# Fourier mixing with three real products for four: a spectral layer's weight stage rewritten

## The chip, the cores and the metric

One core of a Trainium2 chip runs the whole program. Its engines work side by side and meet through semaphores: TensorE (PE, matmul, with its weight loads listed apart as PEld), VectorE (DVE), ScalarE (ACT), GpSimd (POOL) and SyncE (SP, which here only issues transfers). The metric is the device time of one execution in microseconds (us); lower is better.

## What is computed

The input is x, 4 batches of 512 times, 128 positions (n) and 64 channels (c), all in float32. Two layers follow each other. Layer 0 (normalisations, a scan, convolutions, a feed-forward block) is not touched. Layer 1, cut to what matters:

```
trend = _moving_average(x, 25)
seasonal = x - trend
xf = rfft(seasonal, axis=time)
xs = xf[:, :128]
W = w_real + 1j * w_imag
ys = einsum('bmnc,cmk->bknc', xs, W)
filt = irfft(ys padded with zeros, n=512)
return trend + filt
```

The `einsum` is the mixing. For each of the 64 channels a complex 128 x 128 matrix W[c] takes the 128 spectral modes m to 128 modes k, for every batch and position. With X = Xr + iXi and W = A + iB the plain form needs four real products: Yr = A.Xr - B.Xi and Yi = B.Xr + A.Xi.

## The kernel before

Layer 1 takes the batches in two pairs (G = 2). For each pair it runs three stages, one after the other: `transform` of both batches (moving average and forward Fourier transform as matmuls), `mix`, and `invert` of both (inverse transform, with the trend added and the result stored). Between the stages lies one large tile, `xf`, with 128 partitions of spectrum; per batch it has two planes r = 0, 1 of 64 x 128 columns. It is permuted so that a fixed channel's columns can be read as matmul input: for one channel, 2 batches x 64 x 2 = 256 columns, in runs of two neighbouring elements.

The spectrum is packed by symmetry classes of the modes. `MODES` lists modes 0, 4, 8, ... (32 of them), then 2, 6, 10, ... (32), then the odd ones (64). After `transform`, plane 0 holds the real parts in this order; plane 1 holds the imaginary parts with its halves turned, the odd modes first (`IMAG` is `MODES` rolled by half). After `mix`, plane 0 holds the even modes in four blocks of 32 (real, imaginary, real, imaginary) and plane 1 the odd ones in two blocks of 64; this packed order is what `invert` multiplies.

`transform` (L987) goes through 16 slabs of 512 columns in 8 groups of two. Per group: loads on SP, sums and differences on VectorE (L1006 to L1010), three small copies to `edge` on ScalarE (L1002), then matmuls L1018 (128 x 64 weights), L1026 (128 x 32 weights, four of them side by side in the array's columns) and L1035, then four ScalarE copies of PSUM to `xf` (L1042).

`mix` (L1044) goes through 16 groups of four channels (CG = 4). Per group it loads 1 MB of weights: for each channel two 128 x 128 matrices for each of two output planes, already arranged on the host so that plane 0 and plane 1 of `xf` are each multiplied once into each output plane. GpSimd flips the signs of a part of them (L1053, two instructions of 128 x 256). Then TensorE runs 16 matmuls of 128 x 128 weights and 256 columns (L1060 and L1064, four per channel), two at a time summed in PSUM, and VectorE and ScalarE copy the sums back over the spectrum in `xf` (`evacuate`, L962 to L966), two instructions of 128 x 256 each per two channels.

`invert` (L1076) goes through 16 slabs per batch, `waves(s)` ahead of `trends(s - 1)`: matmuls L1086 and L1088 into four PSUM banks, VectorE sums L1094 and L1098, then matmuls L1114 and L1117 and four VectorE sums L1120, and a store from GpSimd's queue (L1121).

TensorE's order is the program's order (`manual_schedule`); the order on the other engines is made by a planner when the program is built. Every float32 matmul stands in the profile as two instructions, so 512 matmuls of the two `mix` stages are 1024 rows. Buffers bind the stages: the `big` pool has five slots of 8 KB per partition, used in turn by input slabs (`xin`) and by weights (`w`); PSUM has eight banks of 512 columns, tag "a" with four and tag "b" with four.

The lines that bind most:

```
1044  def mix(xf):
1049      w = slabs.tile([P, CG, 2, 2, M], F32, tag="big", name="w", bufs=5)
1050      nc.sync.dma_start(w, wri[:, g * CG : (g + 1) * CG, :, :, :])
1056      py = [bank("b"), bank("b")]
1129  with tc.manual_schedule(engines={nc.tensor.engine}):
1134      mix(xf)
```

Of the kernel before, what the change touches and what calls it, by code (L numbers as in the profile page):

```python
# [31 lines left out]
TURN = 16  # L32

MODES = np.concatenate([np.arange(0, M, 4), np.arange(2, M, 4), np.arange(1, M, 2)])
IMAG = np.roll(MODES, H)

HALVES = np.arange(D).reshape(-1, 2, 2, 2, H)
HALVES[:, 1] = HALVES[:, 1, :, ::-1].copy()
# [880 lines left out]
def layer1(ctx, tc, x4, wri, dftv, dftd, dfte, idfte, idfto, avg, avgh, out, after):  # L919
# [41 lines left out]

    def evacuate(i, dst, src):  # L962
        if i % 2:
            nc.scalar.copy(dst, src)
        else:
            nc.vector.tensor_copy(dst, src)  # L966

    def slab(b, s):
        xin = slabs.tile([P, NT, SL], F32, tag="big", name="xin", bufs=5)
# [17 lines left out]
    def transform(b, xf):  # L987

        for g in range(NS // 2):
            edge = io.tile([P, SL], F32, tag="edge", name="edge")  # L990
            uv, ev, pf = [], [], []
            for k in range(2):
                s = 2 * g + k
                c = slice(s * SL, (s + 1) * SL)
                with behind(b, s, after["sync"][min(s, 4) + 2]):
                    xin = shifted_slab(b, s)
                ends = xin[0 : 2 * TURN, 0, :]
                if k == 0:
# [8 lines left out]
                nc.vector.tensor_tensor(u, xin[:, 0:2, :], xin[:, 2:4, :], ALU.add)  # L1007
                t = io.tile([P, 2, SL], F32, tag="ev", name="ev")
                for i, op in enumerate((ALU.add, ALU.subtract)):
                    nc.vector.tensor_tensor(t[:, i, :], u[:, 0, :], u[:, 1, :], op)  # L1010
                uv.append(v)
                ev.append(t)
                pf.append([bank("ab"[g % 2]), bank("ab"[g % 2])])
            for k in range(2):
                for i in range(2):
                    for r in range(2):
                        h = 1 - r
                        nc.tensor.matmul(  # L1018
                            pf[k][r][h * H : (h + 1) * H, :], lhsT=dftd_sb[:, i, r, :], rhs=uv[k][:, i, :],
                            start=(i == 0), stop=False,  # L1020
                        )
            for k in range(2):
                for i in range(2):
                    for r in range(2):
                        q = r * H + i * H // 2
                        nc.tensor.matmul(  # L1026
                            pf[k][r][q : q + H // 2, :], lhsT=dftv_sb[:, i, r, :], rhs=ev[k][:, i, :],
                            start=True, stop=False,
                        )
            for k in range(2):  # L1030
                for r in range(2):
                    at = slice(k * H + 32 * r, k * H + 32 * r + 2 * TURN)
                    for h in range(2):
                        hs = slice(h * H, (h + 1) * H)
                        nc.tensor.matmul(  # L1035
                            pf[k][r][hs, :], lhsT=dfte_sb[at, hs], rhs=edge[at, :] if k + r else first,
                            start=False, stop=True,
                        )
            for k in range(2):
                s = 2 * g + k  # L1040
                for r in range(2):
                    nc.scalar.copy(by_c(xf[:, r, s * SL : (s + 1) * SL]), by_n(pf[k][r]))  # L1042

    def mix(xf):  # L1044

        xc = xf.rearrange("p b r (a c l) -> p b r a c l", c=H, l=2)
        for g in range(H // CG):

            w = slabs.tile([P, CG, 2, 2, M], F32, tag="big", name="w", bufs=5)
            nc.sync.dma_start(w, wri[:, g * CG : (g + 1) * CG, :, :, :])  # L1050
            w4 = w[:, :, 1, 0, :].rearrange("p c (n i m) -> p c n i m", n=2, i=2)[:, :, :, 0, :]
            for t in (w4, w[:, :, 1, 1, 0:H]):
                nc.gpsimd.tensor_scalar(t, t, -1.0, 0.0, ALU.mult, ALU.add)  # L1053
            for q in range(CG // 2):
                c0 = g * CG + 2 * q
                py = [bank("b"), bank("b")]
                for r in range(2):
                    for j in range(2):
                        o = py[r][:, j * G * NF : (j + 1) * G * NF]
                        nc.tensor.matmul(  # L1060
                            o, lhsT=w[:, 2 * q + j, 0, r, :], rhs=xc[:, :, 0, :, c0 + j, :], start=True,
                            stop=False,
                        )
                        nc.tensor.matmul(  # L1064
                            o, lhsT=w[:, 2 * q + j, 1, r, :], rhs=xc[:, :, 1, :, c0 + j, :],
                            start=False, stop=True,
                        )
                for r in range(2):
                    for b in range(G):
                        evacuate(  # L1070
                            b,
                            xc[:, b, r, :, c0 : c0 + 2, :],
                            py[r].rearrange("p (c b a l) -> p b a c l", c=2, b=G, l=2)[:, b],
                        )

    def invert(b, xf):  # L1076

# [2 lines left out]
        def waves(s):  # L1080

            c = slice(s * SL, (s + 1) * SL)
            ev, od = [bank("a"), bank("a")], [bank("a"), bank("a")]
            for h in range(2):
                hs = slice(h * H, (h + 1) * H)
                nc.tensor.matmul(ev[h], lhsT=idfte_sb[hs, :], rhs=xf[hs, 0, c], start=True, stop=True)  # L1086
            for i in range(2):
                nc.tensor.matmul(od[i], lhsT=idfto_sb[:, i, :], rhs=xf[:, 1, c], start=True, stop=True)  # L1088
            even = io.tile([P, 2, SL], F32, tag="ev", name="even")
            two = io.tile([P, SL], F32, tag="even", name="two")  # L1090
            nc.scalar.copy(two, ev[1])  # L1091
            halves[s] = []
            for i, op in enumerate((ALU.add, ALU.subtract)):
                nc.vector.tensor_tensor(even[:, i, :], ev[0], two, op)  # L1094
            for i in range(2):
                pm = (slabs if i else io).tile([P, 2, SL], F32, tag=f"uv{i}", name="pm")
                for k, op in enumerate((ALU.add, ALU.subtract)):
                    nc.vector.tensor_tensor(pm[:, k, :], even[:, i, :], od[i], op)  # L1098
                halves[s].append(pm)

        def trends(s):
# [3 lines left out]
            for j in range(NT):  # L1105
# [22 lines left out]

    with tc.manual_schedule(engines={nc.tensor.engine}):
        for b0 in range(0, B, G):  # L1130
            xf = spec.tile([P, G, 2, D], F32, tag="xf", name="xf")
            for b in range(G):
                transform(b0 + b, xf[:, b, :, :])
            mix(xf)
            for b in range(G):
                invert(b0 + b, xf[:, b, :, :])


def _constants():
# [43 lines left out]
def _inputs(x, i):  # L1183
# [18 lines left out]
            wconv[sa, q, 2 * H :] = taps[2 - 2 * a]  # L1202


    planes = []
    for rows, parts in ((MODES, ("w_real", "w_imag")), (IMAG, ("w_imag", "w_real"))):
        w = [i[n][:, rows][..., MODES] for n in parts]
        planes += [[v[..., q : q + H // 2] for q in (0, H // 2) for v in w], [v[..., H:] for v in w]]
    wri = np.stack([np.concatenate(p, axis=2) for p in planes], axis=2)
    b = x.shape[0]  # L1210
    a = {
        "x": x.reshape(b, T, D),
# [11 lines left out]
        "wri": wri.reshape(H, M, 2, 2, M).transpose(1, 0, 2, 3, 4),  # L1224
        **_constants(),
    }
    return {n: np.ascontiguousarray(v) for n, v in a.items()}
# [17 lines left out]
```

## Time and profile before

| | us |
|---|---|
| median of 3 runs | 3674.95 (3670.21 to 3675.77) |
| the profiled execution | 3668.25 |
| its span (first to last instruction) | 3666.5 |
| first `mix`: first matmul to the first matmul of `invert` | 2816.30 to 2927.74 |
| second `mix`: the same | 3298.44 to 3409.9 |
| first `transform` stage, its matmuls | 2699.4 to 2814.0 |
| first `invert` stage, its matmuls | 2927.7 to 3172.9 |

Over the whole span TensorE is busy for 94%, VectorE 74%, ScalarE 49% and GpSimd 12%. These shares are averages over stages with different limits, so the stages are looked at one by one. In the tables of groups, a row gives line, engine, operation, output and inputs, shapes, count, then busy time in us and the mean duration of one in ns, then the idle time before them and what ended it. In the timeline a row gives the start, the duration of the whole run of equal instructions, and the count after "x". A matmul's duration is longer than the distance to the next one, because matmuls are pipelined: for what a stage costs, the distance between starts counts.

### The profile page before, as it was taken

The numbers are of one execution on the slowest core, as the hardware profiler recorded it, in microseconds if no ns is written. First come the engines' busy times: TensorE is split into PE (matmuls) and PEld (weight loads), VectorE is DVE, ScalarE is ACT, GpSimd is POOL, SyncE is SP. The second block draws the span as 40 slices with busy tenths as digits, with TensorE's granted clock in tenths as the row PEclk, the third lists the DMA queues.
The fourth block names the chain that finished last, engine by engine and source line by source line (L and its number), as shares of the span: only waits on it lengthen the run. The fifth ranks groups of instructions, "written<-read, shape, count | busy, mean of one in ns | idle before, by whom it ended". The sixth has DMA issues, their size and how long they took to land. (4 is left out here: it accounts for less than half of the span.)

```text
span 3666.5 us, 53980 instructions
## 1 busy us (share of the span) xinstructions
PE 3458.3 (94%) x20297; PEld 1363.8 (37%) x20297; DVE 2707.6 (74%) x3530; ACT 1787.3 (49%) x2363; POOL 448.6 (12%) x657
## 2 busy tenths in 40 slices
PE   8989998889998899999899989999999999999998
PEld 3433332234333223433322333343334833328433
DVE  4476779976776996677699799956677277892677
ACT  0013445655666565666656688878864200252100
POOL 0000012210111211010122121100001000001000
PEclk9999999999999999999999999999999999999999
DMA  9876657787885788788478678646668478994688
GB/s 314 288 260 232 225 187 257 257 280 269 288 275 174 265 275 289 271 282 282 164 264 284 214 255 266 227 169 213 233 197 266 149 254 289 300 302 148 224 281 263
DMA packets 427732, 910.48 MB, mean 248 GB/s; under 512 B 32848, under 2 KB 83664, under 8 KB 423376
## 3 DMA queue, kind: packets, MB, share of 16 engines
q1 hardware_dynamic: 353904, 637.11, 53.3%
q0 software_dynamic: 71680, 268.46, 20.3%
q8 instruction: 162, 2.65, 0.3%
q10 hardware_dynamic: 1888, 1.45, 0.1%
q14 instruction: 98, 0.80, 0.1%
HBM read 638.39 MB, written 268.50 MB: 247 GB/s over the span
## 5 line engine op out<-in xcount | busy, mean ns | idle before, releaser
L780 PE MATMUL p<-mid,w_sb 64*64 64x512 f32 x2048 | 551.5, 596 | 17.6 <-DVE wx L793 17.6
L780 PE MATMUL pb<-mid,w_sb 64*64 64x512 f32 x2048 | 534.0, 596 | 0.0
L770 ACT ACTIVATE mid<-c,fb_sb 128x1024 f32<-128x1024 f32 x256 | 284.3, 1111 | 93.0 <-PE c L765 90.8
L770 ACT ACTIVATE mid<-m,fb_sb 128x1024 f32<-128x1024 f32 x256 | 284.6, 1112 | 92.0 <-PE m L765 90.8
L765 PE MATMUL c<-x,w_sb 64*64 64x512 f32 x2016 | 279.0, 606 | 12.8 <-ACT mid L770 6.5
L765 PE MATMUL m<-x,w_sb 64*64 64x512 f32 x2016 | 283.0, 613 | 7.4 <-ACT ob L814 5.0
L780 PEld LDWEIGHTS p<-mid,w_sb 64*64 64x64 f32 x2048 | 154.1, 134 | 291.9 <-issue 262.1
L1091 ACT COPY two<-a 128x512 f32<-128x512 f32 x64 | 37.5, 585 | 432.0 <-PE a L1086 432.0
L414 PE MATMUL a<-xp,wx 128*128 128x512 f32 x512 | 235.2, 603 | 0.5 <-DVE me L269 0.5
L1114 PE MATMUL b<-xin,avg_sb 128*128 128x512 f32 x512 | 230.8, 593 | 3.3 <-DVE xin L1120 3.3
L1120 DVE TENSOR_TENSOR xin<-b,pm 128x512 f32<-128x512 f32 x256 | 159.1, 683 | 101.3 <-PE b L1117 86.3
L601 ACT ACTIVATE sq<-x 128x1024 f32<-128x1024 f32 x128 | 135.0, 1055 | 156.9 <-DVE x L596 156.8
L252 PE MATMUL st<-x,ones 128*32 128x512 f32 x512 | 185.2, 611 | 24.5 <-DVE x L596 24.5
L656 DVE SCALAR_TENSOR_TENSOR to<-kd,vec,to 128x511 f32<-128x511 f32 (+1 forms) x272 | 196.9, 742 | 10.4 <-ACT to L652 8.1
L733 ACT ACTIVATE kd<-kd,vec 128x512 f32<-128x512 f32 x256 | 192.7, 803 | 3.1 <-DVE kd L725 3.1
L966 DVE COPY xf<-b 128x256 f32<-128x256 f32 x128 | 54.3, 424 | 179.0 <-PE b L1060 170.0
L542 DVE TENSOR_TENSOR x<-a,xp 128x1024 f32<-128x1024 f32 x128 | 156.0, 1219 | 38.2 <-PE a L538 35.6
L656 DVE SCALAR_TENSOR_TENSOR z<-x,vec,z 128x511 f32<-128x511 f32 x240 | 175.6, 744 | 5.0 <-ACT z L652 3.6
L736 DVE TENSOR_TENSOR x<-kd,kx 128x1024 f32<-128x1024 f32 x126 | 154.0, 1222 | 33.4 <-ACT kd L733 33.4
L538 PE MATMUL a<-rst,wo_sb 64*64 64x512 f32 x1024 | 143.3, 627 | 27.5 <-DVE x L542 25.2
L793 DVE SCALAR_TENSOR_TENSOR x4t<-p,fb_sb,x 128x512 f32<-128x512 f32 x64 | 47.7, 746 | 160.0 <-PE pb L780 157.6
L724 DVE TENSOR_TENSOR kd<-kh,rm 128x1024 f32<-128x1024 f32 x128 | 155.6, 1219 | 7.1 <-ACT rm L286 4.6
(275 smaller groups left out, 6773.5 us busy)
## 6 DMA issues: line engine op xcount, KB each, us to landing
xp<-in_xt SPq DMA_DIRECT2D x256, 512.0 KB
kh<-to SPq DMA_DIRECT2D x156, 512.0 KB
x<-x POOLq DMA_DIRECT2D x128, 512.0 KB, 4.4
kx<-x SPq DMA_DIRECT2D x128, 512.0 KB
x<-ob POOLq DMA_DIRECT2D x64, 1024.0 KB, 8.1
xin<-x SPq DMA_DIRECT2D x64, 1024.0 KB
out<-xin POOLq DMA_DIRECT2D x64, 1024.0 KB, 6.3
x<-x SPq DMA_DIRECT2D x96, 512.0 KB
```

The lines of the kernel that those rows point to most:

```text
L252: nc.tensor.matmul(st[32 * q : 32 * q + 32, :], lhsT=ones, rhs=src[:, j, :], start=first, stop=last,)
L414: nc.tensor.matmul(pa[:, k, :], lhsT=wq[:, j, k * P : (k + 1) * P], rhs=xp[:, j, :], start=first and j == 0, stop=last and j == 1,)
L542: nc.vector.tensor_tensor(x1, at, xp, ALU.add)
L656: tap = nc.vector.scalar_tensor_tensor(to[:, j, k:], xr[:, j, : SL - k], vec[:, w, c], to[:, j, k:], ALU.mult, ALU.add)
L724: nc.vector.tensor_tensor(d, to, pair_of(rb), ALU.mult)
L733: tc.keep_in_program_order(nc.scalar.activation(d[:, j, :], d[:, j, :], AF.Identity, bias=vec[:, B4, c], scale=vec[:, G4, c]))
L736: nc.vector.tensor_tensor(x3, d, x2, ALU.add)
L765: nc.tensor.matmul(pm[halves[j], h, :], lhsT=w1_sb[halves[h], q * H : (q + 1) * H], rhs=x3[halves[h], j, :], start=True, stop=True,)
L770: gelu = nc.scalar.activation(mid, pm, AF.Gelu_apprx_tanh, bias=fb1_sb[:, q : q + 1])
L780: nc.tensor.matmul(sums2[i][j][halves[h], :], lhsT=w2_sb[halves[j], q, :], rhs=mid[halves[j], h, :], start=q == 0, stop=q == 3,)
L1114: nc.tensor.matmul(po[j], lhsT=avg_sb[:, j, :], rhs=xin[:, j, :], start=True, stop=False)
L1120: nc.vector.tensor_tensor(by_n(xin[:, j, :]), by_n(po[j]), by_c(pm[j % 2][:, j // 2, :]), ALU.add)
```

## The change

The complex product is written with three real products per channel: with d = Xr - Xi (formed by VectorE), B.d is common to both results, and (A - B).Xr + B.d = Yr and (A + B).Xi + B.d = Yi. The parts, in words:

- The host gives the two real planes of W only, 512 KB per group of four channels. GpSimd forms A - B and A + B into two further planes of the same tile (two instructions of 128 x 512 per group), in place of the sign flips.
- `xf` holds the real part in plane 0 and the imaginary part in plane 1, with modes in the same order in both; the order of its dimensions becomes plane, batch, column. `transform`'s last copies turn the halves of plane 1: one ScalarE copy of 128 partitions and two of 64 per slab, for two of 128.
- `mix` has four steps per group: `load_weights`, `differ` (d, one VectorE instruction of 128 x 1024 elements), `common` (four matmuls with 128 x 128 weights, then five ScalarE copies and one VectorE copy that lay the result out in the packed order, as `first` and `other`) and `own` (32 matmuls with 128 x 32 weights, each to 32 partitions of PSUM, in sets of four that differ in these partitions, then two VectorE sums of 128 x 1024 which write `xf` in the packed order that `invert` reads). They are issued so that `common` of the next group stands ahead of `own` of this one.
- PSUM is taken in pairs of banks everywhere in layer 1 (`banks`, two per tag, for `bank`, four per tag), so two neighbouring banks are taken and given back together.

```diff
-    ps = ctx.enter_context(tc.tile_pool(name="ps", bufs=4, space=PSUM))
+    ps = ctx.enter_context(tc.tile_pool(name="ps", bufs=2, space=PSUM))
...
-    def bank(tag):
-        return ps.tile([P, SL], F32, tag=tag, name=tag)
+    def banks(tag):
+        return ps.tile([P, 2, SL], F32, tag=tag, name=tag)
...
                 s = 2 * g + k
-                for r in range(2):
-                    nc.scalar.copy(by_c(xf[:, r, s * SL : (s + 1) * SL]), by_n(pf[k][r]))
+                c = slice(s * SL, (s + 1) * SL)
+                nc.scalar.copy(by_c(xf[:, 0, c]), by_n(pf[k][:, 0, :]))
+                for h in range(2):
+                    rows, turned = slice(h * H, (h + 1) * H), slice((1 - h) * H, (2 - h) * H)
+                    nc.scalar.copy(by_c(xf[rows, 1, c]), by_n(pf[k][turned, 1, :]))
...
+        def by_a(block):
+            return block.rearrange("p k (c a l) -> p a (k c) l", c=2, l=2)
+
+        def load_weights(g):
+            w = ws[g] = slabs.tile([P, 4, CG, M], F32, tag="big", name="w", bufs=5)
+            nc.sync.dma_start(w[:, 0:2], wri[:, g])
+            nc.gpsimd.tensor_tensor(w[:, 2], w[:, 0], w[:, 1], ALU.subtract)
+            nc.gpsimd.tensor_tensor(w[:, 3], w[:, 0], w[:, 1], ALU.add)
+
+        def differ(g):
+            d = ds[g] = slabs.tile([P, CG, G * NF // 2, 2], F32, tag="uv1", name="d")
+            c = channels(g)
+            nc.vector.tensor_tensor(d.rearrange("p c a l -> p a c l"), xc[:, 0, :, c, :], xc[:, 1, :, c, :], ALU.subtract)
+
+        def common(g):
+            w, d = ws[g], ds.pop(g)
+            pk = banks("a")
+            for c in range(CG):
+                nc.tensor.matmul(
+                    pk[:, c // 2, c % 2 * G * NF : (c % 2 + 1) * G * NF], lhsT=w[:, 1, c, :], rhs=d[:, c], start=True, stop=True
+                )
+            first = io.tile([P, 2, SL], F32, tag="uv0", name="first")
+            other = io.tile([P, 2, SL], F32, tag="ev", name="other")
+            q = H // 2
+            for at in range(4):
+                nc.scalar.copy(first[at * q : (at + 1) * q], pk[at // 2 * q : (at // 2 + 1) * q])
+            nc.scalar.copy(other[0:H], pk[H:P])
+            nc.vector.tensor_copy(other[H:P], pk[H:P])
+            turns[g] = first, other
+
+        def own(g):
+            w = ws.pop(g)
+            q = H // 2
+            parts = (((0, 0), (1, 0), (0, 1), (1, 1)), ((0, 2), (0, 3), (1, 2), (1, 3)))
+            py = [banks("b"), banks("b")]
+            for k in range(2):
+                for c in range(CG):
+                    for at, (r, m) in enumerate(parts[k]):
                         nc.tensor.matmul(
+                            py[k][at * q : (at + 1) * q, c // 2, c % 2 * G * NF : (c % 2 + 1) * G * NF],
+                            lhsT=w[:, 2 + r, c, m * q : (m + 1) * q], rhs=xc[:, r, :, g * CG + c, :],
+                            start=True, stop=True,
                         )
+            for k, turn in enumerate(turns.pop(g)):
+                nc.vector.tensor_tensor(xc[:, k, :, channels(g), :], by_a(py[k]), by_a(turn), ALU.add)
+
+        for g in range(3):
+            load_weights(g)
+        differ(0)
+        common(0)
+        differ(1)
+        for g in range(NG):
+            if g + 3 < NG:
+                load_weights(g + 3)
+            if g + 1 < NG:
+                common(g + 1)
+            if g + 2 < NG:
+                differ(g + 2)
+            own(g)
...
-            ev, od = [bank("a"), bank("a")], [bank("a"), bank("a")]
+            ev, od = banks("a"), banks("a")
...
-            po = [bank("b") for _ in range(NT)]
+            pairs = [banks("b"), banks("b")]
+            po = [pairs[j // 2][:, j % 2, :] for j in range(NT)]
```

More of the change, by code (lines that the diff above doesn't have):

```diff
@@ L960, in by_n @@
         return row.rearrange("p (a l c) -> p a l c", c=H, l=2)
[L962 to L966, printed above, removed]
     def slab(b, s):
@@ L1012, in transform @@
                 ev.append(t)
-                pf.append([bank("ab"[g % 2]), bank("ab"[g % 2])])
+                pf.append(banks("ab"[g % 2]))
             for k in range(2):
@@ L1035, in transform @@
                         nc.tensor.matmul(
-                            pf[k][r][hs, :], lhsT=dfte_sb[at, hs], rhs=edge[at, :] if k + r else first,
+                            pf[k][hs, r, :], lhsT=dfte_sb[at, hs], rhs=edge[at, :] if k + r else first,
                             start=False, stop=True,
@@ L1040, in transform @@
                 s = 2 * g + k
-                for r in range(2):
-                    nc.scalar.copy(by_c(xf[:, r, s * SL : (s + 1) * SL]), by_n(pf[k][r]))
-    def mix(xf):
[L1046 to L1059, printed above, removed]
+                c = slice(s * SL, (s + 1) * SL)
@@ L1082, in waves @@
             c = slice(s * SL, (s + 1) * SL)
-            ev, od = [bank("a"), bank("a")], [bank("a"), bank("a")]
+            ev, od = banks("a"), banks("a")
             for h in range(2):
                 hs = slice(h * H, (h + 1) * H)
-                nc.tensor.matmul(ev[h], lhsT=idfte_sb[hs, :], rhs=xf[hs, 0, c], start=True, stop=True)
+                nc.tensor.matmul(ev[:, h, :], lhsT=idfte_sb[hs, :], rhs=xf[hs, 0, c], start=True, stop=True)
             for i in range(2):
-                nc.tensor.matmul(od[i], lhsT=idfto_sb[:, i, :], rhs=xf[:, 1, c], start=True, stop=True)
+                nc.tensor.matmul(od[:, i, :], lhsT=idfto_sb[:, i, :], rhs=xf[:, 1, c], start=True, stop=True)
             even = io.tile([P, 2, SL], F32, tag="ev", name="even")
             two = io.tile([P, SL], F32, tag="even", name="two")
-            nc.scalar.copy(two, ev[1])
+            nc.scalar.copy(two, ev[:, 1, :])
             halves[s] = []
             for i, op in enumerate((ALU.add, ALU.subtract)):
-                nc.vector.tensor_tensor(even[:, i, :], ev[0], two, op)
+                nc.vector.tensor_tensor(even[:, i, :], ev[:, 0, :], two, op)
             for i in range(2):
@@ L1130, in layer1 @@
         for b0 in range(0, B, G):
-            xf = spec.tile([P, G, 2, D], F32, tag="xf", name="xf")
+            xf = spec.tile([P, 2, G, D], F32, tag="xf", name="xf")
             for b in range(G):
-                transform(b0 + b, xf[:, b, :, :])
+                transform(b0 + b, xf[:, :, b, :])
             mix(xf)
             for b in range(G):
-                invert(b0 + b, xf[:, b, :, :])
+                invert(b0 + b, xf[:, :, b, :])
 def _constants():
@@ L1202, in _inputs @@
             wconv[sa, q, 2 * H :] = taps[2 - 2 * a]
[L1205 to L1209, printed above, removed]
+    wri = np.stack([i[n][:, MODES][..., MODES] for n in ("w_real", "w_imag")], axis=1)
     b = x.shape[0]
```

27 lines of the change are left out of this document (9 added, 18 removed).

## The prediction

> **What bounds the kernel now.** I read the busy shares by stage first, because the change touches layer 1 alone. In this view the columns are the stretch, its length, busy time (count) of PE, PEld, DVE, ACT, POOL, then the granted clock, the DMA share and GB/s.
>
> ```profile
> core 0: us, PE busy (x) PEld busy (x) DVE busy (x) ACT busy (x) POOL busy (x), PEclk, DMA share, GB/s
> 2760.00:2790.00 30.00, 27.19 (x198) 7.82 (x194) 29.05 (x35) 17.49 (x30) 0.00 (x0) 1.00 1.01 290
> 2816.00:2928.00 112.00, 111.61 (x514) 95.86 (x516) 27.04 (x64) 24.11 (x65) 10.06 (x26) 1.00 0.44 152
> 3050.00:3100.00 50.00, 49.93 (x158) 18.75 (x160) 39.97 (x66) 4.09 (x7) 4.51 (x6) 1.00 0.88 289
> ```
>
> Transform (first row) has VectorE at 97% and the DMA engines full; ScalarE is at 58%. Mix (second row) is TensorE alone: never idle, VectorE and ScalarE at a quarter, the clock full. Invert (third row) has TensorE and DMA near their ends. Then the timeline inside mix, for the distance between matmuls:
>
> ```profile
> 2850.35 0.59 PE L1060 MATMUL b<-xf,w 128*128 128x256 f32 x2
> 2850.79 0.59 PE L1064 MATMUL b<-xf,w 128*128 128x256 f32 x2
> 2851.22 0.59 PE L1060 MATMUL b<-xf,w 128*128 128x256 f32 x2
> ```
>
> Four instructions start in 0.87 us: 0.217 each. A group of four channels is 16 matmuls, 32 instructions, 6.94 us; 16 groups are 111.0 us, and the stage takes 111.4 (2816.30 to 2927.74). So what TensorE loses here comes off the end, until another engine needs as long.
>
> **TensorE in the changed mix.** `common`: 4 matmuls of the same form, 8 x 0.217 = 1.74 us a group. `own`: 32 matmuls of 32 weight columns, in sets of four with different output partitions. Their like is L1026:
>
> ```profile
> 2724.32 1.92 PE L1026 MATMUL b<-ev,dftv_sb 128*32 128x512 f32 x16
> ...
> 2724.77 0.13 PEld L1026 LDWEIGHTS b<-ev,dftv_sb 128*32 128x32 f32 x4 [0.30 <-issue]
> 2725.20 0.13 PEld L1026 LDWEIGHTS b<-ev,dftv_sb 128*32 128x32 f32 x4 [0.30 <-issue]
> ```
>
> 16 instructions take four steps of 0.43 us, so four run at once; their four weight loads take 0.13 together, which also fits under a step of half the columns, 0.217. 64 instructions in 16 steps: 3.47 us. Sum 5.21 a group, 83.3 a stage. The other bound, no overlap at all, is 64 x 0.217 = 13.9; the row has the same shape but for the columns, so I take 3.47.
> [...]
>
> **The other engines per group, against 5.21.** Prices:
>
> ```profile
> L814 ACT COPY ob<-m 128x1024 f32<-128x1024 f32 x62 | 62.1, 1001 | 62.4 <-PE m L801 62.4
> L542 DVE TENSOR_TENSOR x<-a,xp 128x1024 f32<-128x1024 f32 x128 | 156.0, 1219 | 38.2 <-PE a L538 35.6
> L1007 DVE TENSOR_TENSOR u<-xin 128x1024 f32<-128x1024 f32 x64 | 76.6, 1218 | 6.4 <-DMA xin<-x 4.8 <-PE c L801 0.8 <-DVE u L1007 0.5
> L966 DVE COPY xf<-b 128x256 f32<-128x256 f32 x128 | 54.3, 424 | 179.0 <-PE b L1060 170.0 <-issue 8.4
> L444 DVE COPY w_sb<-psum_w 66x259 f32<-66x259 f32 x1 | 0.4, 416 | 0.0
> ```
>
> ScalarE: five copies of 1024 elements from PSUM. L814 alone takes 1.00; in a row they overlap (four L1042 of 0.65 take 2.13 below, a step of 0.49), so 0.92 to 1.00 each, 4.6 to 5.0 a group. VectorE: `differ`, one copy, two sums, all 1024 elements: 1.20 to 1.22 each by L1007 and L542 (64 of L1007 are 76.6 us busy), 4.8 to 4.9. Strides are free in these rows: L966, in runs of two elements, takes what the plain L444 takes. Were they not, 4 x 0.424 for a copy would be the other end, 1.70 and 6.8 a group; I take 1.20. GpSimd: two instructions of 512 elements with two inputs. Nearest is L1053, 0.77 for two of 256 with one input; so 0.77 each as the low end, and twice that, 1.54, as the high: 1.5 to 3.1 a group, hidden in either case. Both PSUM pairs of `own` come free in time: a sum must end before its bank is written again 3.47 us later (the other half and `common`) and takes 1.2. `own` waits for `first`, copied 3.9 us after `common`, while 6.9 us of TensorE lie between. SyncE issues as many weight loads, each of half the bytes, in a stage with DMA at 0.44: nothing. So TensorE keeps the lead, but by 0.2 to 0.4 us only where it had three quarters.
>
> **The shared wait of GpSimd and VectorE.** In the transform's end GpSimd stands still while VectorE works on two SBUF inputs:
>
> ```profile
> 2807.42 5.42 POOL L1053 TENSOR_SCALAR w<-w 128x256 f32<-128x256 f32 x4 [107.04 <-DMA w<-in_wri]
> 2815.12 0.77 POOL L1053 TENSOR_SCALAR w<-w 128x256 f32<-128x256 f32 x2 [2.27 <-DMA w<-in_wri]
> ...
> 2808.98 2.49 DVE L1010 TENSOR_TENSOR ev<-u 128x512 f32<-128x512 f32 x4
> ```
>
> Four take 5.42 there, two 0.77 later. Of the new VectorE work only `differ` has both inputs in SBUF. GpSimd can spare the 1.2 us. The trace shows no VectorE instruction held by GpSimd; if one is, `differ` waits up to one instruction, 0 to 1.54 a group, VectorE then needs 4.8 + 1.54 = 6.3, and the price is (6.3 - 5.2) x 32 = 35 us. By the phases they miss each other: `differ` of each round becomes free with the end of a `common`, at 1.9 to 3.2 us after the end of an `own`; the weights that this `own` gives room for land later (before: slot free at 2851.0, GpSimd starts at 2856.1 with 1 MB; half the bytes, 3 to 5 us) and are done by 7. I take a slip of 0.1 a group for all meetings, 3.2 us in two stages.
> [...]
>
> **Start, end and the other stages.** Start: the first matmul of mix began when three of these four copies were done:
>
> ```profile
> 2814.63 2.13 ACT L1042 COPY xf<-b 128x512 f32<-128x512 f32 x4 [4.73 <-PE b L1035]
> ...
> 2816.30 0.70 PE L1060 MATMUL b<-xf,w 128*128 128x256 f32 x2 [1.68 <-ACT xf L1042]
> ```
>
> Now six copies must end (five steps of 0.49 and 0.65: 2817.8), then `differ` 1.2: TensorE starts at 2819.1, 2.8 late. GpSimd, held up till VectorE's transform work ends, may still be forming the first sums then: 0 to 1.5, I take 0.6. End: L1086 reads plane 0, whose sum ends under the second half of `own`; L1088 waits for the last sum, 0.2 + 1.2 after TensorE instead of today's 1.06: 0.4. A stage thus takes 83.3 + 2.8 + 0.4 = 86.5 for 111.4: gain 24.9, two stages 49.8. Pairs of banks in invert: `od` of the second slab now waits for four L1098 sums instead of two, 1.2 us later, once at each of four batch starts (0 to 4.8, I take 2.4, half, since invert also waits for DMA); in the steady order the sums are done 1.7 us ahead. Transform: two more ScalarE copies per group, 1.0 us, on ScalarE at 58%; VectorE and DMA hide them. The chain there (six copies 3.4, three edge copies 1.9) ends 5.3 after the matmuls, and L1035 asks at 5.9; without that margin it would be 1 us in each of 32 groups.
>
> Sum: 49.8 - 1.2 (GpSimd at two starts) - 3.2 - 2.4 = 43.0. The profiled execution, 3668.25 (span 3666.5 and 1.75 around it), becomes 3625.3. The median is 6.7 higher, so I forecast 3674.95 - 43.0 = 3632.
>
> **Rivals.** (1) VectorE or ScalarE sets the pace: `differ` held each round, strided reads that cost, or copies at L770's 1.11 (5.6 a group). At 4.8 + 1.15 = 5.95 a group (GpSimd midway between its prices) the gain shrinks by 0.74 x 32 = 24, of which 3 are in the sum: 3652; at 6.3, 3664. For it: three engines within 10% of each other. Against: the phases above, and L966. Chance 0.20. (2) Slower: the sets of four in `own` do not run together at 256 columns, since 8 instructions must start in 0.217 us. Two at a time make 6.94 + 1.74 = 8.7 a group, 139 + 3.2 a stage, 31 us more for each: 3737; none, 3958. It loses from 0.63 us a step on ((111.4 - 3.2) / 16 - 1.74 = 5.02, over 8 sets of two steps), against 0.43 for a set. Against: L1026's loads and matmuls start 7 ns apart. Chance 0.08. (3) The gain is given back because invert waits for DMA anyway: its input slabs are loaded into slots that the weights free, so they move with mix; five are ahead at its start, as today. It would leave half, 3653. Chance 0.04.
>
> **How the numbers follow.** The forecast has 0.68, with its own range 3619 to 3645: below, the full 49.8 and the 5.6 by which the runs spread; above, a slip of 0.4 a group and invert's 4.8 in full. The range takes in most of (1) and (3): 3619 to 3657. Differences below 0.2%, 7 us, can't be told from none. Slower 0.08 from (2); within 0.2%, 0.03, the far end of (1); faster 0.89.
>
> **What would show it.** In the profile after: sets of four `own` matmuls 0.22 us apart (by twos, or 0.3 and more: rival 2); 5.2 to 5.3 us from group to group in mix and mix some 87 long; TensorE idle there less than 5% (VectorE above 97% and TensorE waiting for `xf` or `d`: rival 1); `differ` at 1.2 us with no gap ahead of it while GpSimd works; transform and invert as long as before within 3 us. The forecast is wrong if a copy of 32 partitions, or a strided sum, costs more than its row here.

## The result, and the profile after

| | before | after |
|---|---|---|
| median of 4 runs, us | 3672.58 (3661.93 to 3675.77) | 3864.82 (3852.83 to 3868.11) |
| the profiled execution / its span | 3668.25 / 3666.5 | 3866.03 / 3863.5 |
| last transform matmul to first `mix` matmul | 2.3, 2.3 | 5.8, 5.8 |
| first to last `mix` matmul | 111.0, 111.0 | 199.5, 198.7 |
| last `mix` matmul to the inverse transform | 0.5, 0.5 | 2.0, 1.8 |
| inverse transform to the second `transform`; to the end of the span | 247.1; 256.6 | 251.3; 259.3 |

The changed kernel is slower: 1.053 times the time before, 95% interval 1.0512 to 1.0548. Of the 197 us between the two spans, 88.5 + 87.7 = 176 lie between the first and the last matmul of the two `mix` stages. The transform is as long as before (112.3 for 114.6, then 120.7 for 121.3).

The view by windows (the columns as before) shows two stretches of the first `mix` after:

```profile
2865.00:3024.00 159.00, 126.96 (x928) 76.81 (x928) 109.17 (x51) 151.20 (x65) 40.76 (x19) 0.94 0.18 57
2830.00:2905.00 75.00, 59.49 (x432) 36.93 (x424) 57.43 (x23) 74.45 (x34) 34.17 (x11) 0.93 0.12 37
```

TensorE, never idle there before, is busy for 80%, and ScalarE, whose five copies should leave it a margin, for 95 to 99%. Is ScalarE then the bound, as rival 1 has it? The timeline of one group says no:

```profile
2953.44 2.82 ACT L1075 COPY other<-a 64x1024 f32<-64x1024 f32 x1
...
2954.19 3.95 PE L1087 MATMUL b<-xf,w 128*32 128x256 f32 x32
...
2955.76 3.24 POOL L1055 TENSOR_TENSOR w<-w 128x512 f32<-128x512 f32 x1 [7.53 <-DMA w<-in_wri]
2956.28 9.29 ACT L1074 COPY first<-a 32x1024 f32<-32x1024 f32 x4
2956.29 2.74 DVE L1076 COPY other<-a 64x1024 f32<-64x1024 f32 x1 [2.24 <-ACT other L1075]
...
2959.06 1.22 DVE L1093 TENSOR_TENSOR xf<-b,other 128x1024 f32<-128x1024 f32 x1
2960.20 4.74 DVE L1061 TENSOR_TENSOR d<-xf 128x1024 f32<-128x1024 f32 x1
...
2960.34 4.07 PE L1087 MATMUL b<-xf,w 128*32 128x256 f32 x32 [2.20 <-DVE xf L1093]
...
2964.34 1.59 PEld L1067 LDWEIGHTS a<-d,w 128*128 128x128 f32 x8 [0.86 <-issue]
2964.34 1.99 PE L1067 MATMUL a<-d,w 128*128 128x256 f32 x8
2964.86 1.21 DVE L1093 TENSOR_TENSOR xf<-b,first 128x1024 f32<-128x1024 f32 x1
```

Two things are seen. A half of `own` (32 instructions, eight sets) takes 4 us instead of eight times 0.217 = 1.74. And most of what another engine has under way beside a half of `own` ends only when that half ends: `differ`, 1.2 us of work, begins at 2960.20 and ends at 2964.94, just after the 32 matmuls, and GpSimd's L1055 takes 3.24 us beside the first half; the sums of L1093, between two halves or after them, take 1.22. (ScalarE's L1075, begun 0.75 us ahead of the matmuls, is held as well, 2.82 us, but ends 2.1 us into them.) The groups say the same as means:

```profile
L1074 ACT COPY first<-a 32x1024 f32<-32x1024 f32 x128 | 271.0, 2118 | 13.6 <-PE a L1067 11.8
L1087 PE MATMUL b<-xf,w 128*32 128x256 f32 x2048 | 255.6, 644 | 62.6 <-DVE xf L1093 61.8
L1061 DVE TENSOR_TENSOR d<-xf 128x1024 f32<-128x1024 f32 x32 | 141.9, 4442 | 19.4 <-ACT xf L1038 14.0 <-PE a L1067 5.4
```

The median of L1074 is 1.002 us, its mean 2.118, its longest 7.93. A copy of the same shape takes 1.00 us or several times that, by what TensorE does beside it. ScalarE is held, not overloaded.

The size: within `own` there are 0.113 us from instruction to instruction, 64 in a group, 7.2 us; with 1.92 for `common` that is 9.15, 146 us in 16 groups. The other 53 of the 199.5 are waits of TensorE, of which the list of waits names 38 in the first stage (its 5.3 for `d` lie ahead of the first matmul):

```profile
PE b L1087 <- DVE xf L1093: 31.4, 16, 3.3
PE a L1067 <- DVE d L1061: 5.3, 1, 5.3
PE a L1067 <- issue: 4.1, 1, 4.1
PE a L1067 <- DVE other L1076: 2.9, 2, 1.6
```

### The profile page after: what moved, and what is told of

It is laid out like the page before. It is cut to its first block, busy times and chain, and to the rows that moved or that the text cites. A ratio compares the mean times of both kernels' runs of the same rounds, so it can differ in the third digit from the quotient of the medians.

```text
span 3863.5 us, 56844 instructions
## 1 busy us (share of the span) xinstructions
PE 3562.1 (92%) x21577; PEld 1371.0 (35%) x21577; DVE 2950.8 (76%) x3530; ACT 2166.5 (56%) x2459; POOL 579.6 (15%) x657
## 3 DMA queue, kind: packets, MB, share of 16 engines
q8 instruction: 172, 2.82, 0.3%
## 5 line engine op out<-in xcount | busy, mean ns | idle before, releaser
L1087 PE MATMUL b<-xf,w 128*32 128x256 f32 x2048 | 255.6, 644 | 62.6 <-DVE xf L1093 61.8
L1074 ACT COPY first<-a 32x1024 f32<-32x1024 f32 x128 | 271.0, 2118 | 13.6 <-PE a L1067 11.8
L1087 PEld LDWEIGHTS b<-xf,w 128*32 128x32 f32 x2048 | 147.0, 130 | 157.1 <-DVE xf L1093 81.8
L598 POOL DMA_DIRECT2D x<-x x128 | 93.5, 730 | 526.0 <-DVE x L595 500.7
```

Of the source, the lines that this page charges most:

```text
L1074: nc.scalar.copy(first[at * q : (at + 1) * q], pk[at // 2 * q : (at // 2 + 1) * q])
L1087: nc.tensor.matmul(py[k][at * q : (at + 1) * q, c // 2, c % 2 * G * NF : (c % 2 + 1) * G * NF], lhsT=w[:, 2 + r, c, m * q : (m + 1) * q], ...
```

## The experiments

All are made from the changed kernel. "Set" is the distance from one `own` instruction to the fourth after it, "group" from one group of four channels to the next (the median).

**What the four streams read.** The theory: a run of two elements at every 512 bytes, four times at once, is more than SBUF gives. Rivals: the step of 512 itself, not the short runs; or the number of instructions and weight loads, whatever they read. The first run lets `own` multiply 256 contiguous columns of the weights, the second runs of two at a step of 64 bytes (both give other data); the third and fourth keep the data and let two streams, or one after the other, run at a time.

```diff
-  rhs=xc[:, r, :, g * CG + c, :]
+  rhs=w.rearrange("p k c m -> p (k c m)")[:, r * 256 : (r + 1) * 256]      # contiguous
+  rhs=(the same row).rearrange("p (n s) -> p n s", s=16)[:, :, 2 * r : 2 * r + 2]      # runs of two, 64 B
-  for c in range(CG): for at, (r, m) in enumerate(parts[k])
+  for pair in ((0, 1), (2, 3)): for c in range(CG): for at in pair      # two streams
+  for at, (r, m) in enumerate(parts[k]): for c in range(CG)      # one stream
```

> The 32-column matmuls of `own` read 256 neighbouring columns of the weight tile in place of the spectrum (so `own` multiplies other data than the reference); all else as in the changed kernel. Theory A (four streams in runs of two elements take up the SBUF reads, so the matmuls slow down and every other engine's SBUF accesses stand still): sets of four 0.22 us apart instead of 0.48, ScalarE copies 1.0 us each and none over 1.2, `differ` 1.2 instead of 4.8, about 5.2 to 5.5 us a group, 3625 to 3660 us. Theory B (it is the step of 512 bytes): the same. Theory C (four matmuls at once of 256 columns are too many instructions, weight loads or PSUM writes): as the changed kernel, 3865 us.

> As the run before, but `own` reads the weight tile in runs of two elements, 64 bytes apart (128 runs). Theory A (short runs): stalls as in the changed kernel, copies of 2 to 8 us beside `own`, 3840 to 3890 us. Theory B (the step of 512 bytes alone): no stall, 3625 to 3660 us. Theory C: 3865 us.

> The spectrum is read as in the changed kernel, but the matmuls of `own` are ordered so that two run at once, not four (same products, same places). Theory A: two streams of runs of two ask for as many short reads as four long ones, so a step of two stays near 0.22 us (3.5 us a half, 6.9 + 1.7 a group), ScalarE copies stay near 1.0 us: 8.7 us a group, 3730 to 3760 us, faster than the changed kernel although TensorE does less at once. If the stall is of a kind that two streams cause as well: over 3865 us with copies over 2 us.

> As the run before with one matmul of `own` at a time. Theory A: 0.217 us an instruction, 13.9 + 1.7 = 15.6 us a group, all copies 1.0 us and `differ` 1.2 us, 3945 to 3975 us. If the stall comes from reading the spectrum in place at all (while VectorE and ScalarE work on it), copies stay long here too.

| | time | group | instruction to instruction | L1074, mean / longest |
|---|---|---|---|---|
| changed kernel | 3864.82 | 12.0 | 0.113 | 2.12 / 7.93 |
| contiguous | 3642.38 | 5.51 | 0.0495 | 1.00 / 1.01 |
| runs of two, 64 B | 3653.42 | 5.78 | 0.0536 | 1.00 to 1.07 |
| two streams | 3718.81 | 7.87 | 0.086 | 1.00 to 1.11 |
| one stream | 3795.66 | 10.05 | 0.123 | 1.00 to 1.01 |

(One run each; the kernel before took 3671.64 on the same chip.) The number of instructions falls as a cause: with the same 64 and contiguous data four really run at once, sets 0.217 apart, and no copy is held (the longest L1074 is 1.01). Short runs alone fall too: at 64 bytes they cost next to nothing (0.0536 us from instruction to instruction for 0.0495). The step of 512 stays. Both reordered runs missed what was expected of them, and for one reason: matmuls that were to follow each other ran beside each other (in "one stream" the 64 of a group took 8.20 us, for 13.9 one at a time). In "one stream" two thus ran at once, on different channels and all but undisturbed (a group 10.05 for the expected 15.6); in "two streams" mostly four did, of which two shared a channel, and they lost a third of their speed (0.288 from set to set; a group 7.87 for 8.7).

**Other channels beside each other.** So the four matmuls of a set were given four different channels, whose reads lie 128 or 8 bytes apart; a control spreads the groups but keeps one channel per set.

```diff
-  return slice(g * CG, (g + 1) * CG)
+  return slice(g, H, NG)      # 128 B and control; weights permuted to match
+  e = (c + at) % CG      # 128 B and 8 B: used for c in lhsT and output, and in
+  rhs=xc[:, r, :, g + NG * e, :]      # 8 B: g * CG + e
```

> The same work, on groups of channels g, g+16, g+32, g+48, with the four matmuls that run together on four different channels, so their reads stand 128 bytes apart modulo the step of 512. Theory 'the streams meet in one part of SBUF' (the two planes are 64 KB apart, so the same channel in both planes and the step of 512 keep every read of a set in one place): sets of four start 0.22 us apart, first copies 1.0 us median and none over 1.5, a group in 5.2 to 5.8, mix 90 to 100, time 3630 to 3665. Theory 'any four streams with a step of 512 bytes are too many' (the step alone is what costs, wherever the streams stand): sets stay at 0.45 to 0.5 us, copies are held as in the changed kernel, time 3850 to 3875.

> The changed kernel's own groups of four neighbouring channels, with the four matmuls that run together on four different channels, so their reads stand 8 bytes apart modulo 512. It tells how wide the part of SBUF is in which streams meet. If it is 8 bytes: sets 0.22 us apart, 3640 to 3665. If 16: two and two meet, 0.28 to 0.3 us a set, period 6.2 to 6.8, 3670 to 3700. If 32 or more: all four meet as in the changed kernel, 0.45 to 0.5 us, 3850 to 3875. Theory 'the step alone': also 3850 to 3875, so it is read together with the run at 128 bytes.

> Control for the run with four channels 128 bytes apart: the same spread groups g, g+16, g+32, g+48, but the four matmuls that run together all read the same channel, as in the changed kernel. Theory 'the streams meet in one part of SBUF': nothing is gained by the spread alone; sets at 0.45 to 0.5 us, 3850 to 3880. If the spread of the groups itself (the sums' and differences' strides, the weights' order) is what helps, this runs as the other does, under 3670.

The control stalls as before (3849.55, set 0.42). Both others are free of the stall (the longest L1074 at 128 bytes is 1.22, the mean at 8 bytes 1.07), but at 0.265 to 0.289 a set and not 0.22: 3682.62 at 8 bytes and 3699.8 at 128 (ratio 1.0078, 1.0052 to 1.0103). For 8 bytes that is what places 16 bytes wide foretold; for 128 bytes my expectation of 0.22 was wrong. So places modulo 512 don't explain the 0.265 to 0.289 at 128 bytes.

**Sixteen patterns in a stage.** In one run every group of both stages read another pattern:

> A measurement of the reads alone: in each of the 16 groups of a stage the 64 own matmuls read another pattern of the spectrum (so the output is other data); the rest of the step is as in the changed kernel. Read is the time from set to set of four, and what happens to the copies beside it. Theory 'place': all reads of a set that fall in one place modulo 512 bytes wait for each other. It expects: planes 0/1 or one plane, same channel, step 512: 0.45 to 0.5 us; streams 16 to 128 bytes apart: 0.22 to 0.29; step 520, 528, 544, 576, 640 (the place walks on): 0.22; step 256: 0.25 to 0.35; step 1024: 0.48 or more; runs of four at 512: 0.25 or less, of eight 0.22, of one 0.9. Two at a time, same channel: 0.288 for two; different channels: 0.22. Theory 'writes': where the sums of four matmuls go decides part of it: contiguous reads with the four results in other columns of PSUM take 0.288 instead of 0.22, and the changed kernel's reads with other columns take less than 0.45. Theory 'number': only the number of runs of two per set counts at steps of 512 and more, wherever they stand: every pattern of runs of two at 512 to 768 takes 0.45 to 0.5.

| what the four streams of a set read (runs of two unless said) | set, us |
|---|---|
| contiguous; the same with the results in other PSUM columns | 0.216; 0.216 |
| step 512 B, one channel: two planes; one plane; two planes, results in other PSUM columns | 0.44 to 0.48; 0.45 to 0.49; 0.46 |
| step 512 B, four channels 8 B apart; 128 B apart | 0.289; 0.289 |
| step 512 B, four channels 16, 32 or 64 B apart | 0.218 to 0.220 |
| one channel, step 16, 32, 64 B | 0.223 to 0.232 |
| one channel, step 128 B; 256 B; 768 B; 1024 B | 0.345; 0.47; 0.465 to 0.487; 0.465 |
| one channel, step 520, 544, 576 B; 640 B | 0.23 to 0.24; 0.345 |
| one channel, step 512 B: runs of eight; of four; of one | 0.216; 0.243; 0.97 |
| ordered two by two (the next block's streams join in): one channel; 128 B apart; 8 B apart | 0.30; 0.30; 0.38 to 0.42 |

None of the three theories held as it stood. 'Writes' failed: other PSUM columns change nothing, neither for contiguous reads (0.216) nor for the changed kernel's (0.46). 'Number' failed: at a step of 512 four channels 16 to 64 bytes apart take 0.22, not 0.45. 'Place' was right but for its 512: a step of 256 takes 0.47 (0.25 to 0.35 expected), one of 640 takes 0.345 (0.22 expected).

What sorts the rows of the table, and all other patterns but one, is the address modulo 256 bytes, in 16 places of 16 bytes; the places are inferred from these times, no row shows one. A set has 4 x 128 = 512 runs. All in one place (steps 256, 512, 768, 1024) they take 0.47, so 0.92 ns a run; 1024 runs of one take 0.97 and 256 runs of four 0.243, both 0.95 ns. Streams 128 bytes apart, at 0, 128, 256 and 384, meet two and two modulo 256, as do those 8 bytes apart; at 16, 32 and 64 each has a place of its own. A step of 640 acts like 128, of 576 like 64. The count of runs is not the whole price, though. With 256 runs in each of two places, 0.95 ns would make 0.243, and measured are 0.289 (streams 8 or 128 bytes apart) and 0.345 (one channel, steps of 128 and 640). So the 0.92 to 0.95 ns a run were measured with one place alone; what comes on top with two stays open. The exception is a step of 528 (0.25 in one half, 0.43 in the other), which the rule would put at 0.22; that stays open too. The kernel before is in line with it: its one stream has 128 runs in 0.217 us, at 0.95 ns each an estimated 56% of that time in one place.

The timeline of this run, TensorE and ScalarE, first one channel in one plane, then 64 bytes apart:

```profile
2849.07 7.81 PE L1135 MATMUL b<-xf,w 128*32 128x256 f32 x64
...
2849.22 7.78 ACT L1075 COPY other<-a 64x1024 f32<-64x1024 f32 x1
...
2891.61 3.73 PE L1135 MATMUL b<-xf,w 128*32 128x256 f32 x64
...
2891.76 4.07 ACT L1074 COPY first<-a 32x1024 f32<-32x1024 f32 x4 [0.42 <-PE a L1067]
```

Above, one copy starts 0.15 us behind the 64 matmuls and ends with them, 7.78 us later; below, four copies of the usual 1.0 fit beside the same number. In this run copies were held where one place had all or most of the runs (with runs of four too, up to 3.2 us, though the matmuls there lost a tenth only, and 1.9 to 2.1 us in the order two by two at 8 bytes). At 0.289 a set the copies took 1.03 to 1.11. That a held copy waits for its own few reads or writes in the full place is inferred; no row shows single accesses.

**The spectrum kept by channel.** Another way out: `xf` as [channel][column], so that `mix` reads 256 contiguous elements; the transform's copies then write single elements at 1024 bytes, or (second) runs of eight.

```diff
-  xf = spec.tile([P, 2, G, D], ...)
+  xf = spec.tile([P, 2, H, G * NF], ...)
+  rhs=xf[:, r, g * CG + c, :]      # own
...
+  nc.scalar.copy(xf[:, 0, :, at].rearrange("p c n -> p n c"), pf[k][:, 0, :].rearrange("p (n c) -> p n c", c=H))
+  nc.scalar.copy(xf[:, 0, :, at], pf[k][:, 0, :].rearrange("p (n c) -> p c n", c=H))      # second
```

> The spectrum is kept by channel, so that mix reads and writes runs of 256 contiguous elements, and the step moves to the transform's copies (1024 bytes between elements written) and to the inverse transform's single stream (runs of two). Both theories: own sets 0.22 us apart, copies in mix 1.0 us, period 5.2 to 5.6, mix 88 to 100 as with contiguous data; time 3630 to 3650 if the copies at 1024 bytes and the inverse transform's reads cost nothing. If four inverse-transform matmuls in runs of two meet as in mix, they go at 0.5 to 1.0 us instead of 0.43 and the time passes 3700.

> The kernel with the spectrum kept by channel, with the transform's copies writing runs of eight elements (32 bytes) at 1024 bytes and reading PSUM at 256 bytes instead, in place of single elements at 1024 bytes. If the 1.07 us of those copies (0.64 in the kernels before) came from the single elements: 0.64 to 0.8 us a copy, the transform's 21 and 13 us come back, mix as long as with contiguous data (98 to 103), time 3640 to 3665. If the step of 1024 bytes or the reading of PSUM costs as much: 1.0 us a copy or more, 3685 to 3710.

The groups of the transform's copies, first kernel and then second (median 3692.55 and 3658.96, ratios 1.0063, 1.0041 to 1.0085, and 0.9981, 0.9971 to 0.9990):

```profile
L1036 ACT COPY xf<-b 128x512 f32<-128x512 f32 x32 | 34.3, 1073 | 0.8
```
```profile
L1036 ACT COPY xf<-b 128x512 f32<-128x512 f32 x32 | 18.8, 586 | 38.0 <-PE b L1028 37.6
```

The condition of the first expectation failed, copies that cost nothing: they take 1.07 us instead of the changed kernel's 0.64, and both transforms get longer. Written in runs of eight they take 0.59, and the first transform is as long as in the kernel before (114.8 us; the second takes 125.5 for 121.3). `mix` takes 97.9 us in both, inside what was expected of the first (88 to 100), and its groups 5.8: more than with contiguous reads of the weights, for a reason that the next section finds.

**The rest of the loss.** By the rule, channels four apart (32 bytes) in one set need no other layout. The second kernel leaves GpSimd's sums out.

```diff
+  return slice(g // 4 * 16 + g % 4, g // 4 * 16 + 16, 4)
+  e = (c + at) % CG ... rhs=xc[:, r, :, g // 4 * 16 + g % 4 + 4 * e, :]
```
```diff
-  nc.gpsimd.tensor_tensor(w[:, 2], w[:, 0], w[:, 1], ALU.subtract)
-  nc.gpsimd.tensor_tensor(w[:, 3], w[:, 0], w[:, 1], ALU.add)
+  nc.sync.dma_start(w[:, 2:4], wri[:, g])
```

> The same work as the changed kernel, in groups of four channels that are four apart, with the four own matmuls that run together on four different channels of the group, so that their reads stand 32 bytes apart. Theory 'sixteen places of 16 bytes' (the pattern runs: place = address modulo 256 in steps of 16 bytes): four places, so sets 0.218 us apart, first copies 1.00 to 1.04, a group 5.4 to 5.8, mix 96 to 101 from the transform's last matmul to the first of the inverse transform, time 3635 to 3655, ratio to the kernel before 0.989 to 0.997. Rival 'real sums spoil it' (in the pattern run the sums wrote neighbouring channels; here they and differ step by 32 bytes): sets 0.22, but differ or sums above 1.5 us in the median and the time over 3660.

> The kernel with reads 32 bytes apart, without GpSimd's two instructions for each group: the planes of sums are loaded as the plain weights a second time (so the output is other data, and as many bytes are loaded as in the kernel before the change). Theory 'TensorE sets the pace': a group stays within 0.1 us (5.4 to 5.6), since the 0.3 us by which it passes the sum of its matmuls lie between common and own, where TensorE waits for nothing that the profile shows; differ falls to 1.23; only the two starts gain, 1 to 5 us together: time 3 to 8 us under the other run of this call. Theory 'GpSimd and VectorE hold each other': the group falls to 5.2 to 5.3 and the time by 8 to 15.

Sets are 0.218 apart (50.6 ns an instruction) and L1074's mean 1.008: the rule held. But the time is 3666.11, ratio 0.9989 (0.9979 to 0.9998), and the groups take 5.8 and 6.2 in turn: an expectation missed. The mark of the rival is there, `differ` at 1.76 in the median, yet not as the cause: without GpSimd's sums it falls to 1.22, and still the groups take 5.8 and 6.2 and the first `mix` 99.8 for 99.9 (3663.33, within the scatter). Both numbers expected of that run, 5.4 to 5.6 and 5.2 to 5.3, were wrong. The timeline of VectorE in the first kernel, and the wait in TensorE's line, showed another cause:

```profile
2869.13 1.22 DVE L1094 TENSOR_TENSOR xf<-b,first 128x1024 f32<-128x1024 f32 x1
2870.45 1.23 DVE L1076 COPY other<-a 64x1024 f32<-64x1024 f32 x1
2871.71 1.54 DVE L1094 TENSOR_TENSOR xf<-b,other 128x1024 f32<-128x1024 f32 x1
...
2873.31 1.95 PE L1088 MATMUL b<-xf,w 128*32 128x256 f32 x32 [0.40 <-DVE xf L1094]
```

`own` ended at 2869.1. Both halves of it read both planes of `xf`, which the sums write over; so even the first sum starts after the second half, and the copy for the next group stands between the two. The next `own`'s second half waits for the second sum, which frees its banks. Two kernels test this: the copy moved behind the sums, and (other data) the sums written to `first` and `other` instead of `xf`.

```diff
-  nc.vector.tensor_copy(other[H:P], pk[H:P])      # in common(g + 1), ahead of own(g)
+  if g + 1 < NG: late(g + 1)      # the same copy, after own(g)
```
```diff
-  nc.vector.tensor_tensor(xc[:, k, :, channels(g), :], by_a(py[k]), by_a(turn), ALU.add)
+  nc.vector.tensor_tensor(by_a(turn), by_a(py[k]), by_a(turn), ALU.add)
```

> The kernel with reads 32 bytes apart, with one line moved: VectorE's copy of the second product (1.23 us) comes after the two sums of the group before and no longer between them. Theory 'in place' (the sums write over the planes that the second half of own still reads, so both come after own's end; the second half of the next own waits for the second sum, and the copy between them adds its 1.23 us): the wait of TensorE for that sum, 12 us in all, goes; a group 5.4 to 5.55 us instead of 5.8; first to last matmul of mix 88 to 94 instead of 99.8; time 3640 to 3656, ratio to the kernel before 0.992 to 0.997. Rival 'TensorE waits for d instead' (the difference then ends later): a group stays at 5.7 to 5.9, time 3657 to 3672.

> The kernel with reads 32 bytes apart, with the sums written back over the product that they read and not into the spectrum (so the output is other data). Theory 'in place': the first sum starts with the end of own's first half, TensorE no longer waits for a sum, a group 5.4 to 5.55, time 3640 to 3656. If what costs is the strided reading of own itself, beside the contiguous run's 5.51: a group stays at 5.8, time 3657 to 3672.

| | first to last matmul of `mix` | group | time | ratio |
|---|---|---|---|---|
| 32 bytes apart | 99.9, 99.8 | 5.8 | 3666.11 | 0.9989 (0.9979 to 0.9998) |
| copy moved | 94.1, 94.5 | 5.62 to 5.67 | 3655.63 | 0.9947 (0.9930 to 0.9964) |
| sums elsewhere | 92.6, 93.2 | 5.58 to 5.64 | 3649.35 | 0.9931 (0.9912 to 0.9950) |
| contiguous reads (above) | 91.0, 91.2 | 5.51 | 3642.38 | one run |

Both steps are as "in place" has it, though the groups stay 0.03 to 0.12 above what I expected and `mix` with the copy moved just above its 94. In the list of waits of the first stage, with 32 bytes, the copy moved and the sums elsewhere:

```profile
PE b L1088 <- DVE xf L1094: 3.7, 7, 1.4
```
```profile
PE b L1087 <- DVE xf L1093: 1.4, 1, 1.4
```
```profile
PE b L1088 <- DVE first L1094: 0.7, 4, 0.2
```

The list names less than was lost. From the last start in `own`'s first half to the first start in its second half, the 16 groups of that stage take 9.8 us in all with 32 bytes, and 3.1 with the copy moved, with the sums elsewhere and with contiguous reads of the weights. The second kernel kept by channel, whose reads are contiguous and whose sums are in place, takes 8.1 there, so it is not the strided reading that costs this. The kernel with the copy moved computes what the changed kernel computes, and is faster than it and than the kernel before:

```profile
2830.00:2905.00 75.00, 74.56 (x956) 47.58 (x958) 70.22 (x53) 68.97 (x69) 38.47 (x22) 1.00 0.37 107
```

TensorE is busy for 99% again; VectorE and ScalarE stand at 94 and 92%.

## Why the prediction was wrong

**The step that failed** is "Their like is L1026 ... I take 3.47". L1026 has the same shape of weights, the same partitions and four at once, and in this it was a good witness: with contiguous reads, or places of their own, sets are 0.217 apart. But its four streams read contiguous columns, and `own`'s read runs of two at 512 bytes, all in one place. That "the row has the same shape but for the columns" left out the access pattern of the input, which the program's `rhs` shows. The measured price is 0.44 to 0.49 for a set instead of 0.217: 7.2 us a group instead of 3.47.

**The second half of the failure** is that the other engines were costed at their own durations, whatever TensorE read beside them. Held beside `own`, ScalarE's 4.6 to 5.0 us a group became almost the whole 12. This made most of the 53 us of waits a stage, and these weigh more than the 35 by which the slower sets alone pass the kernel before (146 for 111). ScalarE's copies L1074 went from 1.00 to as much as 7.93 us beside `own`'s reads, and back to a mean of 1.008 with reads 32 bytes apart.

**"Strides are free in these rows"** (by L966) was right of a single stream (0.217 us an instruction in the kernel before) and of VectorE's sums where no `own` ran beside them (1.22 us), and said nothing of four streams at once. It failed again in an experiment, where writes of single elements at 1024 bytes cost 1.07 for 0.64.

**Rival 2** had the right sign and the right sight (sets 0.3 apart and more), and its bound of 0.63 for two steps was passed (twice 0.47). Its mechanism did not happen: the first four of a half start 7 ns apart, and the later ones drift apart but overlap. Its price of 3737 left the held engines out.

**The PSUM pairs that "come free in time"**: wrong, and hidden under the greater loss. The sum waits for `own`'s second half, because it writes in place. Once the reads have places of their own this is 99.9 to 92.6, some 7 us a stage, of which moving the copy brings back 5.8.

**Right, or wrong by a little.** `common` takes 1.92 for 1.74 and `own` at best 3.59 for 3.47, with gaps of 0.3 to 0.4 between the two which the profile puts to no wait: 0.3 a group, 4.8 a stage, not in the sum. The start of `mix` is 3.5 later (2.8 + 0.6 forecast), the end 1.3 to 1.5 (0.4). Not in the sum either: ahead of the first `mix` TensorE stood still for 5.3 us (1.7 before), and then the first 16 instructions of `common` take 6.10 us in the run with contiguous reads, some 2.3 more than at steps of 0.217. In the changed kernel, after as long a standstill, the granted clock reads 0.50 from 2824.3 to 2826.0 us (1.00 from 2816 to 2818 in the kernel before), and six of the first steps take 0.43 us. GpSimd's sums take 1.28 alone and 2.26 when they meet `differ`, which is then 1.7 to 2.3 itself: they meet in most groups, not seldom as forecast, but in the one kernel that leaves the sums out nothing on TensorE's path got shorter. The transform took the two copies for nothing, as forecast. The inverse transform is 2.7 to 4.2 us longer per stage, where 1.2 was forecast; it was not taken apart.

Without the meeting of the streams the forecast of 43 us stands against 29 measured with contiguous reads and 19 in the kernel that computes the same.

## What to carry to other kernels

When matmuls are put side by side, compare their moving reads, not only their shape: count the separate runs of a set for each 16 bytes of the address modulo 256. Here each took 0.92 to 0.95 ns with all in one place; 256 in each of two took 0.289 and 0.345 us a set, for 0.243 by this count. A single stream, by that estimate at 56% of a place, went at 0.217 us an instruction with TensorE never idle; four of the same kind took 0.44 to 0.49 us a set for 0.217, and ScalarE, VectorE and GpSimd were held beside them (up to 8.17, 9.09 and 9.05 us). Give streams that run together different places (here another channel per stream) before changing a layout; and where sums write in place, ask which later reads they must wait for.

## What the runs showed of the hardware that was not expected

- Four streams with one place in common took 0.44 to 0.49 us a set for 0.216, also where all four read the very same addresses (one channel, one plane); with 16 to 64 bytes between them, 0.218.
- In the changed kernel's `mix`, copies from PSUM on ScalarE took up to 8.17 us for 1.01 (L1075), VectorE's `differ` up to 9.09 for 1.23, GpSimd's sums up to 9.05 for 1.28.
- The granted clock read 0.93 to 0.94 in the first `mix` of the changed kernel and 1.00 in the one with the copy moved. Why stays open; 6 to 7% of the clock are not the doubling of a set, 0.44 to 0.49 for 0.217.
